# FFN norm with the halves of the channels added on GpSimd, and the constant places of q and k set on GpSimd

## The chip, the cores and the metric

The kernel runs on one core of a Trainium2 chip. All of its arithmetic is fp32. The metric is the device time of one execution in microseconds; the median of several executions is compared. The core's engines are TensorE (PE, with its weight loads as PEld), VectorE (DVE), ScalarE (ACT), GpSimd (POOL) and SyncE (SP), which here only issues DMAs.

## What is computed

The input `x` has 2 sequences of 2048 tokens with 256 channels. It is normalized over the channels, and the result goes through two branches; the output is `x + s * silu(g)`. Cut to what matters:

```python
xn = layernorm(x)
s = global_attention(xn)              # 16 heads of 16, softmax over all 2048 keys, spatial bias
g = silu(ffn_branch(xn))
out = x + s * g

def ffn_branch(x):                    # two layers of:
    x = x + local_attention(shift_token(x)) @ wo      # 8 heads of 64, windows of 128, rotary q and k
    h = shift_token(x)                # second half of the channels comes from the token before
    mu, var = h.mean(-1), h.var(-1)
    h = (h - mu) / sqrt(var + 1e-5) * lg + lb
    a, gate = split(h @ w1 + b1)
    x = x + (a * gelu(gate)) @ w2 + b2
```

The change touches the mean and the variance of `h` in the FFN, and, in the global attention, the places of the q and k tiles that no data fills.

## The kernel before

The program has two stages. `global_attention` comes first; the first product of `ffn_branch` (L736) starts at 1911.0 us.

**Global attention.** The input comes in chunks of 512 tokens, four for each sequence. `xn_pieces` normalizes a chunk (statistics on VectorE, the root on ScalarE for the first sequence, L234) and turns it over on TensorE into `xA[b]`, which holds channels in partitions: `[128, 2, 2049]`, two halves of 128 channels, with a zero column ahead of the tokens. `prep_qk` multiplies by `wk` and `wq`, writes the product to device memory, and `fetch` brings it back so that each head of 16 channels has 32 partitions of its own in `kTs` and `qTs`. Of these 32, 16 hold data. The places between must hold constants: in `kT` a one in place 16 of each 32, against which the maximum is subtracted, and elsewhere zero; in `qT` zero. `set_rest(i)` (L171 to L174) sets a whole pair of tiles before data arrive, by two ScalarE copies of 128x2048, and fills `vs[i]` with ones on GpSimd. The one comes from `ones_col`, a column loaded by a DMA on ScalarE's queue (L154). `set_rest(0)` stands ahead of the first chunk's statistics, `set_rest(1)` after the last chunk's products. Each engine executes its instructions in the order in which the program issues them. ScalarE's queue at the start thus has the DMAs of constants and weights, then `set_rest(0)`, then the first chunk's root. A DMA issue on these queues can wait until an earlier DMA has ended, since they take eight semaphores in turn.

**FFN branch.** The work is cut into 16 slots: two layers, four chunks of 512 tokens, two sequences, in turn. A slot has four tiles of 128 tokens, and one pass of the outer loop (L1050 on) handles one tile. In each pass the pieces go out in an order written by hand:

```python
STEP = "T0 T1 Q S0 S1 V K F G W0 W1 G A0 A1 G".split()
```

Q, K and V are the projections of the current tile. T turns over q and k of the tile before, S scores them, W turns over the weights and A sums with v. G are pieces of the FFN's first matmuls and gates (`f_gate`), of the slot two before. F holds the other pieces of the pass, `xs`: in pass 0 the variance of the slot two before (`f_var`), in pass 1 the projection and residual of the attention of the slot before (`a_out`), in passes 2 and 3 the FFN's output of the slot three before (`f_out`), and in pass 3 the mean of the slot before (`f_mean`). The first nine passes have another order, in which the attention of each tile is finished one pass later. `soon(n, f)` puts a piece off until n further pieces have gone out. It is used where another engine needs time first.

The mean is a matmul with `mean_w`, a 128x128 matrix of 1/256, which gives the sum over partitions on every partition. The two halves of channels are summed in PSUM, two matmuls each for mean (L903) and variance (L917):

```python
for k in range(2):
    nc.tensor.matmul(pm, mean_w, hs[k], start=(k == 0), stop=(k == 1))
```

VectorE then subtracts `pm` from both halves into `hc` (L906), ScalarE squares them into `sq` (L910), and `f_var` sums the squares. The root of the variance (L920), its reciprocal in four pieces (L927) and two scalings per half (L932, L933) follow on ScalarE and VectorE, spread over later pieces.

GpSimd in this stage adds the rotated halves of q and k (L758), takes the power for their norms (L767) and applies it (L768), scales the attention's weights (L840), prepares the rotary tables (L587), and forms the output in layer 2 (L1028, L1029).

Of the kernel before, what the change touches and what calls it, by code (L numbers as in the profile page):

```python
# [11 lines left out]
F32 = mybir.dt.float32  # L12
AF = mybir.ActivationFunctionType
ALU = mybir.AluOpType
AX = mybir.AxisListType
PSUM = bass.MemoryType.PSUM

B, N, D = 2, 2048, 256
P = 128
NT = N // P  # L20
CH = 512
# [5 lines left out]
NG, GH, HD, HP = 4, 4, 16, 32  # L27
NPR, PH = 2, 8
VW = HD + 1
VALL = (PH - 1) * VW + HP  # L30
# [106 lines left out]
def global_attention(tc, t, xA, s_all, s_out, ident, eps_t, x_ch, early):  # L137
# [9 lines left out]
    nc = tc.nc  # L147
    with ExitStack() as ctx:
        cp = ctx.enter_context(tc.tile_pool(name="ga_c", bufs=1))
        p2 = ctx.enter_context(tc.tile_pool(name="ga_2", bufs=2))  # L150
        psr = ctx.enter_context(tc.tile_pool(name="ps_r", bufs=1, space=PSUM))

        ones_col = cp.tile([P, 1], F32, name="ones_col")
        nc.scalar.dma_start(ones_col, t["ones"][:, 2 * P :])  # L154

        w, padded = {}, {}
        for n in ("wk", "wq", "wv"):
# [4 lines left out]
                padded[n, k] = x  # L162
        for n, k in padded:
            nc.gpsimd.tensor_copy(w[n][:, k].rearrange("p (h d) -> p h d", d=HD), padded[n, k][:, :, :HD])

        qTs = [cp.tile([P, N], F32, name=f"qT{i}") for i in range(2)]
        kTs = [cp.tile([P, N], F32, name=f"kT{i}") for i in range(2)]
        vs = [cp.tile([P, NT, VALL], F32, name=f"v{i}") for i in range(2)]
        zero = xA[0][:, 0, 0:1]

        def set_rest(i):  # L171
            nc.scalar.copy(kTs[i], ones_col.to_broadcast([P, N]))
            nc.scalar.copy(qTs[i], zero.to_broadcast([P, N]))
            nc.gpsimd.memset(vs[i], 1.0)  # L174

        dram = ctx.enter_context(tc.tile_pool(name="qk_d", bufs=1, space=bass.MemoryType.DRAM))
        qk_d = {}
# [312 lines left out]
        def both(a, b):  # L490

            n = max(len(a), len(b))
            for i in range(n):
                for x in (a, b):
                    for f in x[i * len(x) // n : (i + 1) * len(x) // n]:
                        f()
# [2 lines left out]
        turns = [firsts[c][0][3:] + firsts[c][1] for c in range(NCH)]  # L499
        preps = [first_preps(c) for c in range(NCH)]  # L500
        maxima = [[(lambda j=j: max_piece(j)) for _ in range(TPC) for j in range(GH)] for _ in range(NCH + 1)]
        set_rest(0)
        both(stat[0], [])
        both(turns[0], stat[1])
        both(preps[0] + turns[1], stat[2])
        both(preps[1] + turns[2], stat[3])
        both(maxima[0], preps[2] + turns[3])
        both(maxima[1], preps[3])
        set_rest(1)
        rest = [lambda: next(sb) for _ in range(4)] + prep[3 * NCH :]  # L510
        both(maxima[2] + maxima[3], rest[:-4])
        both(maxima[4][: LEAD * GH], [lambda: others.pop(0)()] + rest[-4:])
# [141 lines left out]
def ffn_branch(tc, t, xA, s_out, weights, ident, eps_t, mean_w, vecs, b2_row, x_ch, out_ch):  # L654
# [7 lines left out]
    nc = tc.nc  # L662
    with ExitStack() as ctx:
        cp = ctx.enter_context(tc.tile_pool(name="ff_c", bufs=1))
        pool = ctx.enter_context(tc.tile_pool(name="ff", bufs=2))
# [12 lines left out]
        def bank(name, shape=(P, CH)):  # L678
            turn[0] += 1
            return psr.tile(list(shape), F32, tag=f"f{turn[0] % 8}", name=name)  # L680
# [4 lines left out]
        def soon(n, f):  # L685
            later.append([n, f])
# [29 lines left out]
        def release(kind, b):  # L716
            if (kind, b) in held:
                cc, h = held.pop((kind, b))
                at = (cc + 1) * CH
                nc.vector.tensor_copy(xA[b][:, 1, at : at + 1], h)  # L720


        slots = [(l, b, cc) for l in range(DEPTH) for cc in range(NCH) for b in range(B)]
# [171 lines left out]

        fs = {}

        def f_mean(s):
            l, b, cc = slots[s]
            hs = [xA[b][:, k, cc * CH + 1 - k : (cc + 1) * CH + 1 - k] for k in range(2)]  # L900
            pm = bank(f"pm_{s}")
            for k in range(2):
                nc.tensor.matmul(pm, mean_w, hs[k], start=(k == 0), stop=(k == 1))  # L903
            hc = pool.tile([P, 2, CH], F32, tag="hc", name=f"hc_{s}")
            for k in range(2):
                nc.vector.tensor_sub(hc[:, k, :], hs[k], pm)  # L906
            release("f", b)
            sq = pool.tile([P, 2, CH], F32, tag="sq", name=f"sq_{s}", bufs=1)
            fs[s] = {"hc": hc, "sq": sq, "u": []}
            soon(1, lambda: nc.scalar.activation(sq, hc, AF.Square))  # L910

        def f_var(s):
            l, b, cc = slots[s]
            hc, sq = fs[s]["hc"], fs[s]["sq"]
            pw = bank(f"pv_{s}")
            for k in range(2):
                nc.tensor.matmul(pw, mean_w, sq[:, k, :], start=(k == 0), stop=(k == 1))  # L917
            rs = pool.tile([P, CH], F32, tag="rs", name=f"rs_{s}", bufs=1)
            def root():
                nc.scalar.activation(rs, pw, AF.Sqrt, bias=eps_t)  # L920
                for q in range(TPC):
                    soon(2 * q + 1, lambda q=q: invert(q))
                soon(2 * TPC + 2, lambda: scale(0))
                soon(2 * TPC + 3, lambda: scale(1))

            def invert(q):
                nc.vector.reciprocal(rs[:, q * P : (q + 1) * P], rs[:, q * P : (q + 1) * P])  # L927

            def scale(k):
                c0 = 2 * NM + k  # L930
                V = vecs[:, l, :]
                nc.vector.tensor_mul(hc[:, k, :], hc[:, k, :], rs)  # L932
                nc.vector.tensor_scalar(  # L933
                    hc[:, k, :], hc[:, k, :], V[:, c0 : c0 + 1], V[:, c0 + 2 : c0 + 3], ALU.mult, ALU.add
                )
                fs[s]["ready"] = k == 1

            gates.append(root)
# [103 lines left out]
        def out_pieces(s, k):  # L1042
            return [(lambda p=p: f_out(s, k, p)) for p in range(2)]

        def gate_pieces(s):
            return [(lambda m=m, n=n: f_gate(s, m, n)) for m in range(NM) for n in (1, 0)][:-1]
# [3 lines left out]
        for n in range(len(tiles) + 4):  # L1050
            s, i = divmod(n, TPC)
# [5 lines left out]
            def have(x):  # L1057
                return 0 <= x < n_slots


            xs = []
            if s == n_slots:
                if i == 1:
                    xs = [lambda: a_out(s - 1, 0), lambda: a_out(s - 1, 1)] + out_pieces(s - 3, 0)
                    xs += [lambda: f_mean(s - 1)]
                    gq += gate_pieces(s - 2)
                elif i == 2:
                    xs = out_pieces(s - 3, 1) + [lambda: f_var(s - 1)]
                elif i == 3:
                    xs = []  # L1070
                else:
                    xs = [lambda: f_var(s - 2)]
                ng = (5, 2, 5, 5)[i]
            else:
                if i == 0 and have(s - 2):
                    xs = [lambda: f_var(s - 2)]
                if i == 1 and have(s - 1):
                    xs = [(lambda k=k: a_out(s - 1, k)) for k in range(2)]
                if i == 1 and have(s - 2):
                    gq += gate_pieces(s - 2)  # L1080
                if i >= 2 and have(s - 3):
                    xs = out_pieces(s - 3, i - 2)
                if i == 3 and have(s - 1):
                    xs = xs + [lambda: f_mean(s - 1)]
                ng = (5, 2, 3, 2)[i]
# [45 lines left out]
        s = n_slots + 1  # L1131
# [104 lines left out]
```

## Time and profile before

| | |
|---|---|
| median of 3 runs | 3373.33 us (3373.11 to 3376.05) |
| profiled execution | 3379.4 us, span 3377.6 us |
| granted TensorE clock, mean | 0.987 |
| busy PE / PEld | 3298.3 us (98%) / 1630.2 us (48%) |
| busy DVE / ACT / POOL | 2313.2 (68%) / 2093.4 (62%) / 1104.9 us (33%) |
| L903, mean, 128x512 | x64 records |
| L917, variance, 128x512 | x64 records |
| HBM read / written | 36.63 / 16.78 MB |

The profile shows one execution. Its lines name the engine, the line of the kernel, the operation, the tile written and the tiles read, and the shape; "x4" counts instructions. "idle before" tells what released an engine after it had stood idle. The busy time of TensorE is modelled at the end of each matmul, since matmuls overlap, so starts are compared where a length matters. A matmul of fp32 operands in the program appears as two records. Queues that issue DMAs have a q behind the name (ACTq).

### The profile page before, as it was taken

Reading aid. Unit: us, or ns where it says so; the run is one execution under the profiler, and the core shown is the slowest. Engines: PE = TensorE matmul, PEld = TensorE weight load, DVE = VectorE, ACT = ScalarE, POOL = GpSimd, SP = SyncE. Lnnn points to the kernel's source line nnn. Section 1 sums busy time; section 2 is a strip of 40 time slices with the busy share of each in tenths; the row PEclk is TensorE's granted clock in tenths of the full one; section 3 lists DMA queues with packets and bytes.
Section 4 is the critical chain, followed back from the end, with each engine's and each line's share of the span. In section 5 each row is a group of like instructions: output and inputs, shape, how many; then the busy total and the mean of one; then the engine's idle time right before and its main releaser. Section 6 shows DMA issues by size and latency. Waiting matters only on the chain. (4 is left out here: it accounts for less than half of the span.)

```text
span 3377.6 us, 55228 instructions
## 1 busy us (share of the span) xinstructions
PE 3298.3 (98%) x21216; PEld 1630.2 (48%) x21216; DVE 2313.2 (68%) x4978; ACT 2093.4 (62%) x4237; POOL 1104.9 (33%) x951
## 2 busy tenths in 40 slices
PE   6999999999999999999999889999999999999999
PEld 3444444444444444444444355555555555666665
DVE  3798788878777777787786266666666666665642
ACT  3477677667776667767777566555555555555552
POOL 2011111111111111111111365555555555556541
PEclk8899999999999999999999899999999999999999
DMA  2100000000000100000000100000000000000001
GB/s 91 53 1 5 23 1 14 14 13 14 7 18 21 46 14 1 3 12 1 1 1 14 64 9 1 7 1 7 1 1 32 1 19 15 20 20 19 20 20 50
DMA packets 40954, 56.95 MB, mean 17 GB/s; under 512 B 10016, under 2 KB 25460, under 8 KB 40692
## 3 DMA queue, kind: packets, MB, share of 16 engines
q1 hardware_dynamic: 38354, 51.05, 4.7%
q8 instruction: 168, 2.75, 0.3%
q10 hardware_dynamic: 1826, 2.12, 0.2%
q14 instruction: 94, 0.77, 0.1%
q0 software_dynamic: 512, 0.26, 0.0%
HBM read 36.63 MB, written 16.78 MB: 16 GB/s over the span
## 5 line engine op out<-in xcount | busy, mean ns | idle before, releaser
L364 DVE TENSOR_REDUCE mx<-pm 128x1 f32<-128x512 f32 x2048 | 1272.9, 683 | 354.3 <-PE ps L397 308.9
L403 ACT ACTIVATE e<-ps 128x512 f32<-128x512 f32 x2048 | 1069.7, 602 | 259.2 <-PE ps L397 180.2
L361 PE MATMUL pm<-kT,qT 32*128 32x512 f32 x4096 | 1166.3, 626 | 3.6 <-DVE mx L364 3.6
L397 PE MATMUL ps<-qa,kT 32*128 32x512 f32 x4096 | 1110.4, 626 | 14.1 <-ACT e L403 14.0
L427 POOL TENSOR_TENSOR o<-o,part 128x512 f32<-128x512 f32 x224 | 283.8, 1267 | 1450.4 <-ACT part L426 1440.1
L361 PEld LDWEIGHTS pm<-kT,qT 32*128 32x128 f32 x4096 | 487.0, 186 | 374.3 <-DVE mx L364 264.1
L397 PEld LDWEIGHTS ps<-qa,kT 32*128 32x128 f32 x4096 | 442.8, 185 | 212.9 <-ACT e L403 141.5
L416 PE MATMUL po<-e,v 128*32 128x512 f32 x4096 | 497.4, 604 | 1.7 <-DVE mx L364 1.7
L736 PE MATMUL pp<-weights,xA 128*128 128x512 f32 x768 | 361.6, 606 | 0.8 <-DVE s L471 0.8
L758 POOL TENSOR_TENSOR rot<-rot,swp 128x512 f32<-128x512 f32 x128 | 166.8, 1303 | 465.3 <-DVE swp L755 464.7
L954 PE MATMUL pg<-hc,weights 128*128 128x512 f32 x640 | 298.5, 597 | 1.1 <-DVE hc L933 1.1
L416 PEld LDWEIGHTS po<-e,v 128*32 128x32 f32 x4096 | 107.8, 110 | 353.4 <-DVE mx L364 182.3
L426 ACT COPY part<-po 128x512 f32<-128x512 f32 x224 | 131.2, 585 | 224.6 <-PE po L416 223.8
L826 ACT ACTIVATE sm<-sm,wmx 128x256 f32<-128x256 f32 (+1 forms) x512 | 249.6, 489 | 5.5 <-DVE wmx L818 4.5
L767 POOL TENSOR_TENSOR rn<-rn,mhalf 128x8 f32<-128x8 f32 x128 | 210.8, 1647 | 97.5 <-DVE rn L766 92.4
L757 ACT ACTIVATE sqq<-pp 128x512 f32<-128x512 f32 x128 | 76.4, 597 | 262.1 <-DVE swp L755 262.1
L840 POOL TENSOR_TENSOR sm<-sm,wls 128x512 f32<-128x512 f32 (+1 forms) x224 | 222.8, 1026 | 12.1 <-DVE wls L832 12.1
L736 PEld LDWEIGHTS pp<-weights,xA 128*128 128x128 f32 x768 | 136.7, 192 | 130.7 <-issue 122.4
L818 DVE CUSTOM_DVE_ANT_0 sm<-ps,mask 128x256 f32<-128x256 f32 (+1 forms) x512 | 181.3, 410 | 1.1 <-PE ps L805 1.0
L954 PEld LDWEIGHTS pg<-hc,weights 128*128 128x128 f32 x640 | 114.9, 190 | 122.8 <-issue 113.2
L786 DVE COPY xT<-pt 128x512 f32<-128x512 f32 x64 | 43.3, 677 | 155.2 <-PE pt L780 155.1
L805 PEld LDWEIGHTS ps<-xT,xT 64*128 64x128 f32 x1984 | 115.8, 188 | 47.9 <-issue 41.8
(157 smaller groups left out, 3520.1 us busy)
## 6 DMA issues: line engine op xcount, KB each, us to landing
s<-in_x_dram SPq DMA_DIRECT2D x8, 512.0 KB, 5.0
qk_wk<-stage_wk SPq DMA_DIRECT2D x16, 256.0 KB, 2.0
kT<-qk_wk SPq DMA_DIRECT2D x128, 32.0 KB, 1.8
qk_wq<-stage_wq SPq DMA_DIRECT2D x16, 256.0 KB, 2.0
qT<-qk_wq SPq DMA_DIRECT2D x128, 32.0 KB, 1.8
s_out<-s SPq DMA_DIRECT2D x8, 512.0 KB, 2.7
s<-s_out SPq DMA_DIRECT2D x16, 256.0 KB, 3.6
x<-in_x_dram SPq DMA_DIRECT2D x16, 256.0 KB, 3.6
```

Source lines behind the costliest of these rows:

```text
L361: nc.tensor.matmul(ps, qT[rows, q0 : q0 + P], kT[rows, c * CH : (c + 1) * CH], start=True, stop=True)
L364: nc.vector.tensor_reduce(mxs[n][:, i * GH + j, c : c + 1], ps, AX.X, ALU.max)
L397: nc.tensor.matmul(ps, kT[rows, kt * P : (kt + 1) * P], qas[n][rows, :], start=True, stop=True)
L403: nc.scalar.activation(e, ps, AF.Exp)
L416: nc.tensor.matmul(pos[n][j * HP : (j + 1) * HP, :], v[:, kt, (r + j) * VW : (r + j) * VW + HP], es.pop((n, kt, j)), start=(kt % 2 == 0), ...
L427: nc.gpsimd.tensor_add(os[n], os[n], part)
L736: nc.tensor.matmul(ps, xA[b][:, k, at : at + P], W["qkv"][:, k, n * INNER : (n + 1) * INNER], start=(k == 0), stop=(k == 1),)
L767: nc.gpsimd.tensor_tensor(rn, rn, mhalf, ALU.pow)
L818: nc.vector.tensor_tensor_reduce(sm[:, x, lo:], pss[r][:, x, lo:], mask[:, lo:], -1.0, 3e38, ALU.add, ALU.min, mx[:, hb, r, x : x + 1],)
L826: nc.scalar.activation(sm[:, x, lo:], sm[:, x, lo:], AF.Exp, scale=-1.0, bias=mx[:, hb, r, x : x + 1], accum_out=ls[:, hb, r, x : x + 1],)
L840: nc.gpsimd.tensor_mul(sm, sm, ls[:, hb, r, :, None].to_broadcast([P, 2, 2 * P - lo]))
L954: nc.tensor.matmul(ps[:mw], W["1"][:, k, at : at + mw], hc[:, k, :], start=(k == 0), stop=(k == 1))
```

## The change

In the FFN's norm, `f_add` adds the two halves of the channels on GpSimd, into the first half of the tile `hc`, one pass ahead of the mean. The mean is then one matmul with `mean_w`. The subtraction writes `hc` as before. Behind the square, GpSimd adds the two halves of `sq` in place, and the variance is one matmul too. In the last passes of the program, `f_add` stands between the attention's residual and the output pieces of the same pass.

At the beginning, `ones_col` is no longer loaded: VectorE sums the columns 16, 48, 80 and 112 of the identity. `qTs[0]` is set by a GpSimd memset, `kTs[0]` by a GpSimd copy of `ones_col`, both ahead of the copies of the weights; `vs[0]` is filled after them. The second pair and `vs[1]` are set on GpSimd too. A first small square root on ScalarE (`root_table`) stands ahead of the DMAs of the weights. In the order of the changed program the second pair follows GpSimd's 16 DMA issues of `wp`. The packed last tile of the FFN (`f_last`) is in both versions.

```diff
         ones_col = cp.tile([P, 1], F32, name="ones_col")
-        nc.scalar.dma_start(ones_col, t["ones"][:, 2 * P :])
+        nc.vector.tensor_reduce(ones_col, ident[:, HD::HP], AX.X, ALU.add)
+        root_table = cp.tile([P, 1], F32, name="root_table")
+        nc.scalar.activation(root_table, eps_t, AF.Sqrt)
+
+        qTs = [cp.tile([P, N], F32, name=f"qT{i}") for i in range(2)]
+        kTs = [cp.tile([P, N], F32, name=f"kT{i}") for i in range(2)]
+        vs = [cp.tile([P, NT, VALL], F32, name=f"v{i}") for i in range(2)]
+        nc.gpsimd.memset(qTs[0], 0.0)
+        nc.gpsimd.tensor_copy(kTs[0], ones_col.to_broadcast([P, N]))
...
         for n, k in padded:
             nc.gpsimd.tensor_copy(w[n][:, k].rearrange("p (h d) -> p h d", d=HD), padded[n, k][:, :, :HD])
-
-        qTs = [cp.tile([P, N], F32, name=f"qT{i}") for i in range(2)]
-        kTs = [cp.tile([P, N], F32, name=f"kT{i}") for i in range(2)]
-        vs = [cp.tile([P, NT, VALL], F32, name=f"v{i}") for i in range(2)]
-        zero = xA[0][:, 0, 0:1]
-
-        def set_rest(i):
-            nc.scalar.copy(kTs[i], ones_col.to_broadcast([P, N]))
-            nc.scalar.copy(qTs[i], zero.to_broadcast([P, N]))
-            nc.gpsimd.memset(vs[i], 1.0)
+        nc.gpsimd.memset(vs[0], 1.0)
+
+        def set_rest():
+            nc.gpsimd.tensor_copy(kTs[1], ones_col.to_broadcast([P, N]))
+            nc.gpsimd.memset(qTs[1], 0.0)
+            nc.gpsimd.memset(vs[1], 1.0)
...
-        set_rest(0)
         both(stat[0], [])
...
-        set_rest(1)
+        set_rest()
...
+        def halves(s):
+            l, b, cc = slots[s]
+            return [xA[b][:, k, cc * CH + 1 - k : (cc + 1) * CH + 1 - k] for k in range(2)]
+
+        def f_add(s):
+            hs = halves(s)
+            hc = pool.tile([P, 2, CH], F32, tag="hc", name=f"hc_{s}")
+            nc.gpsimd.tensor_add(hc[:, 0, :], hs[0], hs[1])
+            fs[s] = {"hc": hc}
+
         def f_mean(s):
             l, b, cc = slots[s]
-            hs = [xA[b][:, k, cc * CH + 1 - k : (cc + 1) * CH + 1 - k] for k in range(2)]
+            hs = halves(s)
             pm = bank(f"pm_{s}")
-            for k in range(2):
-                nc.tensor.matmul(pm, mean_w, hs[k], start=(k == 0), stop=(k == 1))
-            hc = pool.tile([P, 2, CH], F32, tag="hc", name=f"hc_{s}")
+            nc.tensor.matmul(pm, mean_w, fs[s]["hc"][:, 0, :], start=True, stop=True)
+            hc = fs[s]["hc"]
             for k in range(2):
                 nc.vector.tensor_sub(hc[:, k, :], hs[k], pm)
...
             soon(1, lambda: nc.scalar.activation(sq, hc, AF.Square))
+            soon(2, lambda: nc.gpsimd.tensor_add(sq[:, 0, :], sq[:, 0, :], sq[:, 1, :]))
...
-            for k in range(2):
-                nc.tensor.matmul(pw, mean_w, sq[:, k, :], start=(k == 0), stop=(k == 1))
+            nc.tensor.matmul(pw, mean_w, sq[:, 0, :], start=True, stop=True)
...
-                    xs += [lambda: f_mean(s - 1)]
+                    xs = xs[:2] + [lambda: f_add(s - 1)] + xs[2:] + [lambda: f_mean(s - 1)]
...
+                if i == 2 and have(s - 1):
+                    xs = [lambda: f_add(s - 1)] + xs
                 if i == 3 and have(s - 1):
                     xs = xs + [lambda: f_mean(s - 1)]
```

## The prediction

> **What bounds the kernel now.** I read the page first for the engine shares and the 40 slices, then the busy time by stretches, then the waits of TensorE in the FFN stage, and last the order of time at the three places that the diff touches: the first 20 us, the statistics steps of one slot, and GpSimd around them.
>
> Busy time by stretches (us, then for PE, PEld, DVE, ACT, POOL the busy us and instruction count, then granted clock, DMA share, GB/s):
>
> ```profile
> 0.00:20.00 20.00, 0.75 (x2) 0.36 (x2) 3.81 (x16) 8.01 (x8) 8.27 (x31) 1.00 0.68 214
> ...
> 2400.00:2700.00 300.00, 300.00 (x1608) 167.31 (x1607) 183.83 (x499) 165.32 (x379) 164.63 (x141) 1.00 0.03 10
> ```
>
> In the FFN stage TensorE is busy in all of the 300 us, at full clock, while VectorE, ScalarE and GpSimd work 55 to 61% of the time; from 2700 to 3000 us it reads alike. A busy PE can hide waits, so I ask for them (us in all, times, longest), from 1950 to 3338 us:
>
> ```profile
> PE pt L780 <- POOL rot L768: 5.8, 4, 2.1
> PE px L889 <- ACT oT L882: 4.6, 2, 3.9
> PE pw L853 <- POOL sm L840: 2.0, 7, 0.3
> PE pg L954 <- DVE hc L933: 1.1, 1, 1.1
> ```
>
> With two entries of 0.2 us that is 13.9 us in 1388 us. What stands in TensorE's queue there is the time: taking a matmul out of it takes out its length, and another engine's extra work is free as long as it does not make one of these rows grow. Now the statistics steps of a slot and their length on TensorE (start us, us):
>
> ```profile
> 2534.05 5.51 PE L995 MATMUL py<-u,w 128*128 128x512 f32 x12
> 2539.49 1.98 PE L903 MATMUL pm<-xA,mean_w 128*128 128x512 f32 x4
> 2541.31 1.88 PE L954 MATMUL pg<-hc,weights 128*128 128x512 f32 x4
> ...
> 2556.75 1.88 PE L917 MATMUL pv<-sq,mean_w 128*128 128x512 f32 x4
> 2558.46 3.60 PE L954 MATMUL pg<-hc,weights 128*128 128x512 f32 x8
> ```
>
> Durations overlap, so the start-to-start time is what a matmul costs: pv's four records take 2558.46 - 2556.75 = 1.71 us, 0.43 each. A 128x512 fp32 matmul of the program is two records (768 records at L736 for 384 matmuls), 0.86 us.
>
> The start is another matter: there TensorE waits for ScalarE, which issues DMAs until 11.5 us and then works through four items before the first square root:
>
> ```profile
> 11.51 1.28 ACT L172 ACT_TABLE_LOAD   x1 [11.51 <-DMA wq<-in_wq_dram]
> 12.80 1.90 ACT L172 COPY kT<-ones_col 128x2048 f32<-128x2048 f32 x1
> 14.60 1.89 ACT L173 COPY qT<-xA 128x2048 f32<-128x2048 f32 x1
> 16.51 1.28 ACT L234 ACT_TABLE_LOAD   x1
> 17.81 0.30 ACT L234 ACTIVATE rs<-mv,eps_t 128x4 f32<-128x4 f32 x1
> ```
>
> VectorE's reciprocal at 18.14 comes after 10.94 us of idle time for that root, and TensorE's first instruction comes at 19.22.
>
> **The change, part by part.**
>
> *Matmuls taken out.* Each of 16 slots loses one of two matmuls in the mean (L903) and one of two in the variance (L917): 32 matmuls, 64 records, at 0.43: 64 x 0.43 = 27.5 us. The group table divides busy time instead: 29.1 us / 60 records = 0.485, or 31 us for 64; 0.43 excludes overlap, so I take it and keep 31 as the upper end.
>
> *GpSimd adds.* Each slot gains two 128x512 fp32 adds. The nearest row is the same operation on the same shape, L758 `rot<-rot,swp`: 1.27 to 1.30 us. So 32 x 1.3 = 42 us more for an engine that works 165 us of 300. In the order of the changed program the first add (`hc`) comes one pass after the attention residual and one pass ahead of the mean's matmul; in place it lies between K's `rot` add and K's `rn`. The slot of 2600 us:
>
> ```profile
> 2601.97 1.26 POOL L758 TENSOR_TENSOR rot<-rot,swp 128x512 f32<-128x512 f32 x1
> 2603.34 1.65 POOL L767 TENSOR_TENSOR rn<-rn,mhalf 128x8 f32<-128x8 f32 x1
> 2605.06 1.04 POOL L768 TENSOR_TENSOR rot<-rot,rn 128x512 f32<-128x512 f32 x1
> ```
>
> Its operand is long ready (the residual ended by 2584), so it waits for nothing. Queued behind it are `rn` and `rot`, which would end at 2607.4 in place of 2606.1; who waits is the transpose `pt`, at 2611.54. Cover: 4 us. Cost nothing; if that cover were gone, 1.3 us in each of 16 slots, 21 us. The second add (`sq`) waits for ScalarE's Square. At 2542.83 + 1.07 the square is done, GpSimd has a table product until 2545.6, so the add ends by 2546.9; behind it the next `rot` add starts at 2552.83, and the variance's matmul at 2556.75. Cover: 6 and 10 us. In layer 2 the output's two products stand ahead of it (3074.43 to 3077.06), so it ends near 3078.3; the matmul is at 3089.37. At the very end (mean at 3294.71, square done at 3301.3) the add ends at 3302.6, the matmul starts at 3306.72 and will start about 1 us earlier: 3 us of cover.
>
> *Where the cover fails.* Slot 0 runs while the other order of pieces holds (until about 2040 us). There Square ends at 2031.87, but the next `rot` add began at 2031.39: with the new add between, the `rot` behind it starts near 2033.2, 1.8 us late, and the transpose at 2043.42 had 3.1 us after `rot` ended at 2040.3. TensorE would come 1.7 us earlier; and `pw` at 2040.67 already stretches to 2.91 us on ScalarE's normalization. I give slot 0 back: 1 us. FFN: 27.5 - 1 = 26.5 us.
>
> *The port.* VectorE's product with two operands in SBUF, `rn<-ss,tiny` (128x8):
>
> ```profile
> 2532.06 0.17 DVE L766 TENSOR_TENSOR rn<-ss,tiny 128x8 f32<-128x8 f32 x1
> ...
> 2539.04 1.27 DVE L766 TENSOR_TENSOR rn<-ss,tiny 128x8 f32<-128x8 f32 x1
> ```
>
> The long one coincides with GpSimd's `rot` add of 2539.03 for its whole length. The Trainium skill says why (SBUF — State Buffer, Who interferes with whom): a VectorE instruction with two SBUF inputs and a GpSimd instruction that reads SBUF block each other, the loser for the winner's whole instruction. That speaks against this change: 32 more GpSimd reads of 1.27 us each can hold VectorE up, to 40.6 us by the rule. By the trace VectorE pays this in every pass already, and TensorE waited for it 1.3 us in all (the row of `hc` above and one of the small entries); at 2603 the next thing TensorE needs of VectorE is the copy of `pw` (2604.90, after 0.98 us of idle; it feeds `po` at 2607.82), so 1.27 us of blocking leaves it 0.3 us late with over 1 us to spare. By the rule alone charged to the end, the FFN stage would be 26.5 - 40.6 = 14 us longer; by the trace nothing. I take nothing.
>
> *The start.* Gone from ScalarE: the DMA of `ones_col` (0.52 us), both copies, the first table load; the root's table load moves ahead of the weight DMAs, with one small root: 1.28 + 0.30. What remains between the last DMA issue and the root is nothing, so 17.81 - 11.51 = 6.3 us are freed, if issuing ends when it did. It ends with `bpr`, which waits for a finished DMA: before for the first of `wq`, after (one DMA fewer in the rotation) for the second of `wk`, which GpSimd took up at 10.48. The weights are issued 1.58 - 0.52 = 1.06 us later. So the root comes between 10.9 and 12.9 us, gain 4.9 to 6.9; I take 5.8. On GpSimd the memset of `qT` (row: 2.13 us for 2416 elements, so 1.8) and the copy of `kT` come ahead of the weight copies; `kT` waits for `ones_col`, reduced on VectorE after the first chunk's statistics, at 7.2. The copy of 2048 is not in the trace: between a memset (1.8) and four 512-element two-operand products (5.1); by the row of the same operation, 0.40 us for 256, 3.2. So the `wk` copies end at 11.3 to 13.1; the first product that needs them stands at 21.92, near 16 after. Cover: 3 us or more. `v`'s memset moves ahead of `wp`'s 8 us of DMA issues, and is done near 18, against 26.9 before; its reader, ScalarE's copy at 29.80, moves to 24. The second `kT`, `qT` (84.17 to 87.87 on ScalarE) follow those issues, done near 34 us, and are first written at about 130. ScalarE's freed 3.8 us at 84 hold up only the bias pieces, for which VectorE idled 0.31 us: 0.3.
>
> Sum: 26.5 + 5.8 + 0.3 = 32.6 us. The profiled execution took 3379.4 (span 3377.6), so 3346.8 by its own time; the median before is 3373.33, 6.1 below it, so 3340.7, said as 3341.
>
> **The rivals.**
>
> *The start's gain does not carry on (0.17).* DMAs are the limit there (68% share), and the weights come later; or the half-speed matmuls of that stage (`pp_wk`, weight loads 0.85 us apart from 22.9 to 25.5, 0.43 after) fall otherwise. Against: after the root all is a chain of ScalarE, TensorE and fetches with no fixed time in it. Then 26.8 is left: 3346.5.
>
> *Half of the FFN gain is given back (0.12).* GpSimd's adds make `pt` and `pw` late (rows L780, L853 above grow). At half, 13 us: 3354.
>
> *Slower: blocking reaches TensorE (0.05).* Mechanism: each GpSimd add takes the port just ahead of VectorE's `rn` or `hc` instruction, VectorE's copies of `pw` and `pt` come late, and TensorE stands. Price: all 32 x 1.27 = 40.6 us, against 27.5 + 6.1 saved: 7 us slower, 3380. It decides only if over 33.6 of the 40.6 us reach TensorE, over 1 us per add. Against: VectorE idles 4.44 us ahead of one transposed copy (2549.61).
>
> *More (0.06).* 31 us of matmuls and 6.9 at the start: 3373.3 - 37.9 = 3335.
>
> That the change does not do what it says is excluded by its order of instructions: each `pm` and `pv` group has one matmul instead of two, and nothing else on TensorE differs.
>
> **The numbers.** My case has 0.60, with a range of its own from 3336 to 3346. A difference under 0.2% (6.7 us) can hardly be told here. Faster by more: all but the slower rival and a thin edge, 0.92; within: 0.03; slower: 0.05. The range from 3332 to 3351 takes in the first rival and the larger gain, and leaves out the half gain and the slower case.
>
> **What would show it.** Right: L903 and L917 at x32 records each; the waits of TensorE in the FFN stage within 5 us of 13.9; the root near 12 us and TensorE's first instruction near 13.5; new GpSimd rows `hc<-xA` and `sq<-sq`, x16, 1.3 us. Wrong: a row of TensorE waiting on `hc` or `sq` from GpSimd, or `pt <- POOL rot` well over 6 us; VectorE's `hc` scaling or `rn` rows longer with TensorE idle behind them; or a first transpose still after 17 us.

## The result, and the profile after

The changed kernel took 3338.97 us (median of 4 runs, 3338.0 to 3347.47), the kernel before on the same chip 3374.53; the ratio is 0.99, 95% interval 0.9883 to 0.9917. The forecast was 3341, in a range from 3332 to 3351. The profiled execution took 3338.83 us, span 3337.0, so it is 40.6 us below the profiled one of before. By the medians the gain is 35.6 us, near the forecast's 32.6, but its parts are not, and one of them was not in the forecast at all. The medians here and below leave out two executions, of 3746.63 us (`before_shift`) and 11060.77 us (the kernel before, in the same session).

First the busy time by stretches of the changed kernel (us, then busy us and count of PE, PEld, DVE, ACT, POOL, then granted clock, DMA share, GB/s):

```profile
0.00:20.00 20.00, 5.47 (x13) 2.83 (x14) 6.23 (x27) 5.23 (x10) 11.33 (x29) 1.00 0.71 211
2400.00:2700.00 300.00, 300.00 (x1634) 167.93 (x1633) 187.36 (x509) 168.88 (x386) 176.75 (x152) 1.00 0.03 10
```

TensorE is still busy in all of the 300 us; GpSimd has gone from 165 to 177. The new and the halved instructions, from the views by tile (ns min/median/max, first and last start):

```profile
L916 PE MATMUL pm<-hc,mean_w x32: 592/592/697, 2007.8 to 3256.2; 128*128 128x512 f32 x32
L924 POOL TENSOR_TENSOR sq<-sq x16: 1262/1270/1279, 2014.3 to 3261.6; 128x512 f32<-128x512 f32 x16
```

The mean has x32 records instead of x64, and an addition takes 1.27 us, as the row of `rot` said. One steady slot in order of time (start us, us):

```profile
2515.17 1.12 PE L916 MATMUL pm<-hc,mean_w 128*128 128x512 f32 x2
2516.13 1.88 PE L967 MATMUL pg<-hc,weights 128*128 128x512 f32 x4
...
2531.57 1.02 PE L930 MATMUL pv<-sq,mean_w 128*128 128x512 f32 x2
2532.43 3.60 PE L967 MATMUL pg<-hc,weights 128*128 128x512 f32 x8
```

The variance now holds TensorE for 2532.43 - 2531.57 = 0.86 us; before it was 1.71. The waits of TensorE from 1950 to 3338 us (us in all, times, longest):

```profile
PE px L893 <- ACT oT L886: 4.6, 2, 3.9
PE pw L857 <- POOL sm L844: 2.9, 9, 0.3
PE pt L784 <- POOL rot L772: 2.9, 2, 2.1
PE pw L857 <- ACT sm L841: 2.0, 1, 2.0
```

With two of 0.2 us that is 12.8 us, against 13.9 before. Here `pw` are the attention's weights as TensorE turns them over, and `sm` the same weights as ScalarE or GpSimd normalizes them; `rot` are q or k after the rotation, `rn` their norms, `pt` are q or k as TensorE turns them over, `po` the sums with v, `px` their projection. No row waits on `hc` or `sq` from GpSimd. But the row of ScalarE's `sm` is new, and it is one wait of 2.0 us. Last, the start on ScalarE:

```profile
12.19 0.34 ACTq L189 DMA_DIRECT2D bet<-in_ln_beta_dram  x1
12.56 0.44 ACTq L191 DMA_DIRECT2D bpr<-in_b_proj_dram  x1
13.06 0.30 ACT L239 ACTIVATE rs<-mv,eps_t 128x4 f32<-128x4 f32 x1 [9.78 <-DMA wq<-in_wq_dram]
```

The root comes as soon as the DMA issues end, but they end at 13.0 us. Split at instructions that both kernels have, the 40.6 us are:

| stretch | before | after | gain | forecast |
|---|---|---|---|---|
| start to first root | 17.8 | 13.1 | 4.7 | 5.8 |
| root to first score (`ps`) | 116.4 | 110.5 | 5.9 | 0.3 |
| first score to first `po` | 17.8 | 17.7 | 0.1 | 0 |
| first `po` to last `po` | 1748.6 | 1743.1 | 5.5 | 0 |
| last `po` to first FFN product | 10.4 | 9.7 | 0.7 | 0 |
| FFN, to the end | 1466.6 | 1442.9 | 23.7 | 26.5 |

So the FFN gave 3 us less than thought, the root 1 us less, and the attention from the root to the last `po`, in which the change was to move nothing beyond the bias pieces, gave 11.5.

### The profile page after: what moved, and what is told of

The parts are those of the page before. It is cut to its first block, busy times and chain, and to the rows that moved or that the text cites. A ratio compares the mean times of both kernels' runs of the same rounds, so it can differ in the third digit from the quotient of the medians.

```text
span 3337.0 us, 55149 instructions
## 1 busy us (share of the span) xinstructions
PE 3261.9 (98%) x21152; PEld 1614.2 (48%) x21152; DVE 2312.9 (69%) x4979; ACT 2085.5 (62%) x4233; POOL 1152.7 (35%) x987
## 5 line engine op out<-in xcount | busy, mean ns | idle before, releaser
L967 PEld LDWEIGHTS pg<-hc,weights 128*128 128x128 f32 x640 | 115.0, 190 | 121.3 <-issue 116.0
```

What stands on the lines that cost most here:

```text
L967: nc.tensor.matmul(ps[:mw], W["1"][:, k, at : at + mw], hc[:, k, :], start=(k == 0), stop=(k == 1))
```

## The experiments

Medians, each with the kernel before on the same chip; the last four columns are from the profile:

| kernel | us | before | ratio (95%) | root | root to score | `po` first to last | FFN |
|---|---|---|---|---|---|---|---|
| start_only | 3368.19 | 3376.23 | 0.9972 [0.9965, 0.9979] | 13.4 | 114.1 | 1744.7 | 1467.2 |
| ffn_only | 3353.14 | 3376.23 | 0.9934 [0.9922, 0.9947] | 18.0 | 116.3 | 1746.9 | 1441.6 |
| after_again | 3344.6 | 3376.23 | 0.9905 [0.9892, 0.9919] | 13.8 | 116.0 | 1741.5 | 1442.9 |
| s0_var2 | 3345.59 | 3376.23 | 0.9909 [0.9896, 0.9923] | 13.3 | 114.5 | 1744.7 | 1443.1 |
| double_adds | 3345.46 | 3377.64 | 0.9898 [0.9881, 0.9914] | 13.6 | 114.7 | 1744.7 | 1442.6 |
| early_root | 3338.77 | 3377.64 | 0.9886 [0.9871, 0.99] | 7.4 | 117.2 | 1742.5 | 1441.5 |
| start_delay | 3346.08, one run | 3377.64 | | 15.7 | 116.1 | 1742.5 | 1441.4 |
| before_again | 3377.15, one run | 3377.64 | | 17.5 | 114.6 | 1748.3 | 1466.7 |
| before_shift | 3373.27 | 3375.65 | 0.9991 [0.9982, 1.0001] | 17.8 | 116.3 | 1744.9 | 1466.8 |
| ones_dma | 3344.09 | 3375.65 | 0.9912 [0.9897, 0.9926] | 12.7 | 110.9 | 1745.3 | 1443.2 |
| fills_act | 3350.59 | 3375.65 | 0.9925 [0.9908, 0.9942] | 17.4 | 114.5 | 1742.0 | 1443.0 |

### The two parts alone, and the whole again

`start_only` is the changed kernel with the FFN's code of before; `ffn_only` has the beginning of before and the changed FFN; `after_again` is the changed kernel once more.

> Only the beginning of the change (constants on GpSimd, root table early); the FFN is as before. Theory A (the beginning is worth its chain of waits and, on top, TensorE's half-speed matmuls that fall away as its work closes up): 10 to 11 us faster than before, ratio 0.997, root near 13 us, first attention score (L397 before) near 123.6 instead of 134.2. Theory B (the prediction's: only the chain, 6.1 us): score near 128, ratio 0.998.

> Only the FFN part of the change. Theory A (slot 0 loses 4 us to a stall and a fallen clock, the other 15 slots gain all of 1.72 us): 23.7 us faster than before, ratio 0.993; the stretch from the first FFN product to the end is 23 to 24 us shorter. Theory B (slot 0 gives back only its own 1 us, the shortfall is spread over all slots): the stretch is 26.5 us shorter, or the shortfall is not at one place.

> The changed kernel once more, on the same chip as the others. If the 5.5 us by which the steady global attention (first weighted sum to last) was shorter in its profile is only the spread between executions, a second profile has that stretch anywhere between 1743 and 1749 us. If the change itself shortened it, it is again 1743.

The parts gained 8.0 and 23.1 us by their medians, together 31.1; the whole gained 31.6 in the same session. They add up, so neither part lives off the other. In `start_only` the first score came at 127.5 us, so the beginning was worth its chain of waits alone (theory B). In `ffn_only` neither theory held: the FFN was 25.0 us shorter, and slots 1 and 14 lost as well as slot 0, as shown below.

The repeat also showed where the first profile is better. From 60 to 120 us the first profile of the changed kernel, and then the repeat:

```profile
60.00:120.00 60.00, 57.14 (x222) 24.53 (x222) 38.83 (x66) 11.57 (x22) 0.00 (x0) 0.94 0.14 49
```

```profile
60.00:120.00 60.00, 57.14 (x205) 24.70 (x205) 35.66 (x60) 10.97 (x21) 0.00 (x0) 0.83 0.13 45
```

Same program, same busy share, but a granted clock of 0.94 against 0.83, and 222 matmuls against 205. One product shows the size, first as it stands in the repeat, then in the first profile:

```profile
65.41 3.78 PE L298 MATMUL pp_wk<-xA,wk 128*128 128x512 f32 x4
```

```profile
62.09 1.99 PE L298 MATMUL pp_wk<-xA,wk 128*128 128x512 f32 x4
```

It takes twice as long where the clock is half. The whole times fall into two groups: `start_only` has 7 of 21 runs from 3361.8 to 3364.0 and 14 from 3367.2 to 3371.0; the changed kernel, with its repeat, has four from 3337.7 to 3339.1 and four from 3344.2 to 3347.5. The mean granted clock of each run parts them in the same way, 0.990 in the quick ones and 0.987 or 0.988 in the others. That the clock is lost between 60 and 120 us is seen in the profiled runs alone. The Trainium skill (TensorE: Matmul & The Clock Gate, Part 1) says that the monitor behind the clock looks through a window that runs free of the program, so one kernel can show different slow counts from run to run; that fits, though no run here shows the window. Of the 5.9 us from root to first score, then, most is how that execution fell: in the other eight profiles with the new start the stretch takes 110.9 to 117.2 us, in the four with the old start 114.6 to 116.4.

### Do the additions cost anything?

`double_adds` issues each of the two new GpSimd additions twice, the second one of the squares into the half that nothing reads any more:

```diff
             nc.gpsimd.tensor_add(hc[:, 0, :], hs[0], hs[1])
+            nc.gpsimd.tensor_add(hc[:, 0, :], hs[0], hs[1])
...
             soon(2, lambda: nc.gpsimd.tensor_add(sq[:, 0, :], sq[:, 0, :], sq[:, 1, :]))
+            soon(2, lambda: nc.gpsimd.tensor_add(sq[:, 1, :], sq[:, 0, :], sq[:, 1, :]))
```

> The change, with both GpSimd adds of each slot done twice (the second square add writes the half of the tile that nothing reads): 32 more adds, 41 us of GpSimd time. Theory A (the adds are covered by GpSimd's idle time and by the distance to their readers): slots 2 to 15 take the same 1.72 us less than before, the stretch from the first FFN product to the end grows by 0 to 3 us, at slots 0 and 1 only. Theory B (the adds reach TensorE through the blocking of VectorE, and the cover is thin): each slot is longer by up to 1.3 us, 10 to 40 us in all.

GpSimd in a steady slot of it:

```profile
2499.93 1.27 POOL L909 TENSOR_TENSOR hc<-xA 128x512 f32<-128x512 f32 x1
2501.27 1.28 POOL L910 TENSOR_TENSOR hc<-xA 128x512 f32<-128x512 f32 x1
...
2525.88 1.28 POOL L925 TENSOR_TENSOR sq<-sq 128x512 f32<-128x512 f32 x1 [0.30 <-ACT sq L924]
2527.23 1.27 POOL L926 TENSOR_TENSOR sq<-sq 128x512 f32<-128x512 f32 x1
```

32 more additions are 41 us of GpSimd work, and the FFN takes 1442.6 us against 1442.9. From one mean to the next every slot but slot 0 takes what it took in `after_again`, within 0.05 us (86.62 in most); slot 0 takes 70.4 against 70.8. So outside slot 0 the cover is real, and there is as much again of it.

### Where the 3 us of the FFN went

From one mean to the next, most slots gained 1.71 to 1.73 us, two matmuls at 0.86. Three did not. I took slot 0 first, since the new wait is there, and left its variance at two matmuls, without the addition of squares:

```diff
-            soon(2, lambda: nc.gpsimd.tensor_add(sq[:, 0, :], sq[:, 0, :], sq[:, 1, :]))
+            if s:
+                soon(2, lambda: nc.gpsimd.tensor_add(sq[:, 0, :], sq[:, 0, :], sq[:, 1, :]))
...
-            nc.tensor.matmul(pw, mean_w, sq[:, 0, :], start=True, stop=True)
+            for k in range(1 if s else 2):
+                nc.tensor.matmul(pw, mean_w, sq[:, k, :], start=(k == 0), stop=(k == 1 or s > 0))
```

> The change, but in slot 0 alone the variance stays two matmuls and GpSimd adds no squares. Theory A (the add of the squares in slot 0, between the queue's rot additions, holds VectorE and ScalarE up until TensorE stands and its clock falls): TensorE's wait for ScalarE's normalized weights near 2022 us goes from 1.96 to under 1 us, the granted clock there stays 1.00, and the time falls by 3.2 us (4.1 lost, less the 0.86 of the matmul put back) against the change: 3335.7. Theory B (the stall there has another cause, the matmul's missing 0.86 us alone): 0.9 us slower than the change or the same.

The whole time did not fall by 3.2 us: 3345.59 against 3344.6, but runs in two groups 7 us apart cannot show so little. In its profile TensorE's wait for ScalarE's `sm` is gone and the clock stays at 1.00, as theory A had it. Slot 0 took 71.0 us, against 72.4 in the first profile of the changed kernel but 70.8 in the repeat, which has the addition too. What differs between those two is a race on VectorE. First the first profile, VectorE and then GpSimd:

```profile
2015.57 1.29 DVE L770 TENSOR_TENSOR rn<-ss,tiny 128x8 f32<-128x8 f32 x1
```

```profile
2014.34 1.27 POOL L924 TENSOR_TENSOR sq<-sq 128x512 f32<-128x512 f32 x1 [2.78 <-ACT sq L923]
2015.57 1.27 POOL L762 TENSOR_TENSOR rot<-rot,swp 128x512 f32<-128x512 f32 x1
```

and then the repeat, in the same order:

```profile
2022.51 0.17 DVE L770 TENSOR_TENSOR rn<-ss,tiny 128x8 f32<-128x8 f32 x1
```

```profile
2021.29 1.28 POOL L924 TENSOR_TENSOR sq<-sq 128x512 f32<-128x512 f32 x1 [2.80 <-ACT sq L923]
2022.53 1.30 POOL L762 TENSOR_TENSOR rot<-rot,swp 128x512 f32<-128x512 f32 x1
```

Where VectorE wins, its product takes 0.17 us. Where it loses it takes 1.29, all of GpSimd's instruction. The maxima on VectorE, then ScalarE's normalization, come 1.1 us late, and TensorE stands before `pw`; the first profile, then the repeat:

```profile
2023.87 3.51 PE L857 MATMUL pw<-ident,sm 128*128 128x128 f32 x16 [1.96 <-ACT sm L841]
```

```profile
2029.48 3.23 PE L857 MATMUL pw<-ident,sm 128*128 128x128 f32 x16 [0.63 <-ACT sm L841]
```

Behind the longer wait the granted clock falls, in all three profiles that have it; the first one:

```profile
2025.00:2030.00 5.00, 5.00 (x21) 3.64 (x21) 1.53 (x3) 4.97 (x11) 0.00 (x0) 0.66 0.00 0
```

In the other ten, with a wait of 0.6 us or none, the clock there is 1.00. The race exists since the change, because the new addition pushes `rot` to the very moment of `rn`: without it (`s0_var2`) `rot` starts 2.5 us ahead of `rn`, with two additions (`double_adds`) 1.4 us behind, and `rn` takes 0.17 us in both. In the profiles it was lost in the changed kernel, `ones_dma` and `fills_act` (slot 0: 72.4 to 72.5 us) and won in `after_again`, `early_root` and `start_delay` (70.8) and in `ffn_only` (71.1): 1.6 us, wait and clock together. In all seven the two starts lie within 0.02 us of each other, and their recorded order does not tell who wins: `rot` is recorded 0.006 us ahead in the changed kernel, but behind by 0.006 and 0.009 in `ones_dma` and `fills_act`, which lost too, and within 0.001 in three that won. And in slot 0 a variance matmul is worth little even with the race won, for TensorE waits for ScalarE there.

Slot 1 gained 0.85 of 1.72, slot 14 0.86. There TensorE, 0.86 us earlier, meets the pace of GpSimd's weight products (`sm`), one in 1.00 us; this is read from the trace, and no run tests it. Slot 1 in `after_again`:

```profile
2088.09 1.16 PE L857 MATMUL pw<-ident,sm 128*128 128x128 f32 x8
2089.59 0.66 PE L857 MATMUL pw<-ident,sm 128*128 128x128 f32 x4 [0.34 <-POOL sm L844]
2090.59 0.66 PE L857 MATMUL pw<-ident,sm 128*128 128x128 f32 x4 [0.34 <-POOL sm L844]
```

Before, the same place had one such wait, of 0.17 us. In slot 14 `pw` and what follows it stretch from 2.77 us (3271.93 to 3274.70) to 3.49. For slot 0 like must be compared with like: it takes 71.35 us in the two profiles of before, but 71.0 in `start_only` and `before_shift`, which have one small VectorE instruction more at their start. With the race won the FFN's change shortens it by 0.2 us (`before` to `ffn_only`, and `start_only` to `after_again`), with it lost it lengthens it by 1.4. So what is given back of 1.72 us a slot is 1.5 or 3.1 us in slot 0, 0.87 in slot 1 and 0.86 in slot 14: 3.2 to 4.8 us, not 1.

The stretch ahead of the first mean, from which no matmul was taken, differs between profiles too, from 113.7 to 115.2 us. `start_only` and `after_again` have it alike, and there the FFN gains 24.2 us; `before` and `ffn_only` give the same 24.2 without that stretch. The 23.7 of the first profile is a lost race and a quick stretch ahead of it.

### The start

`early_root` takes the first root off the weights: `wv` is loaded on SyncE's queue, and `gam`, `bet` and `bpr` behind the input there. `start_delay` puts three ScalarE copies of 128x512 ahead of the first root.

```diff
-                nc.scalar.dma_start(x, t[n][:, k].rearrange("p (h d) -> p h d", d=HP))
+                (nc.sync if n == "wv" else nc.scalar).dma_start(x, t[n][:, k].rearrange("p (h d) -> p h d", d=HP))
...
+        for v, n in ((gam, "ln_gamma"), (bet, "ln_beta"), (bpr, "b_proj")):
+            nc.sync.dma_start(v, t[n][None, :].to_broadcast([P, D]))
```

```diff
...
+        for _ in range(3):
+            nc.scalar.copy(delay, eps_t.to_broadcast([P, CH]))
         both(stat[0], [])
```

> The change, with the DMAs of wv, gamma, beta and the projection's bias issued on SyncE's queue instead of ScalarE's. Theory A (after the change the root waits for nothing but the queue's last DMA issues, which wait for the weights to land): the root comes when VectorE's statistics are done, near 7.5 us instead of 13.1 to 13.8; TensorE's first transpose near 9 us; its first product then waits for wk near 12.5 us instead of starting at 17.2: 4 us gained there, if wq and wv land in time. Theory B (the transfers bound the start, 3.5 MB at the rate they have): the products move by under 1 us.

> The change, with three ScalarE copies of 128x512 (about 1.5 us, to a tile that nothing reads) put back ahead of the first root. Theory A (from root to first attention score the time hangs on where TensorE's half-speed stretches fall, 110.5 to 116.4 us in the profiles so far): root 1.5 us later, and the first score anywhere from 125 to 132 us. Theory B (a fixed chain, 110.5 us): the first score 1.5 us after 123.6 to 129.8, and root to score within 0.5 us of the change's own.

> The kernel before once more. If the half-speed stretches of the start fall by chance from execution to execution, root to first score (116.4 us in the first profile and 116.3 in the run with the old start) can be shorter here, down to 110; if they belong to the old order of work, it is 116 again. The steady attention stretch is expected between 1741 and 1749 us.

In `early_root` the root comes at 7.40, 5.7 us earlier, and the first score only at 124.6. In the four profiles with the changed start and a clock of 0.83 to 0.85 from 60 to 120 us it comes at 127.5 to 129.8, in the two with 0.94 (the changed kernel's first and `ones_dma`) at 123.6. The first product shows what stops it:

```profile
11.02 1.89 POOL L163 COPY kT<-ones_col 128x2048 f32<-128x2048 f32 x1 [6.65 <-DVE ones_col L155]
12.86 0.74 POOL L173 COPY wk<-wk 128x256 f32<-128x256 f32 x2
13.31 3.78 PE L295 MATMUL pp_wk<-xA,wk 128*128 128x512 f32 x4 [1.72 <-POOL wk L173]
```

TensorE waits for `wk`, behind the copy of `kT` on GpSimd, which waits for `ones_col`; VectorE makes that at 10.81 us now, among the second chunk's statistics, instead of 7.11. The cover for GpSimd's work at the start is used up. All four runs lie between 3338.58 and 3338.86. Against 3344.6 of the changed kernel's repeat that is better by 6 us, against its first median no difference; the intervals of the two ratios overlap (0.9871 to 0.99, and 0.9892 to 0.9919 for the repeat), so it is not shown to be quicker. It is the steadiest of the versions, in four runs. `start_delay` moved the root by 2 us, and its one run, 3346.08, lies among the changed kernel's slower four, so it cannot tell its two theories apart. `before_again` repeats the kernel before: 114.6 us from root to score, 1.8 less than the first profile of the same kernel, and 1748.3 from first to last `po`, against 1748.6.

`fills_act` gives ScalarE its copies back, for both pairs, and keeps the rest of the new start:

```diff
-        nc.gpsimd.memset(qTs[0], 0.0)
-        nc.gpsimd.tensor_copy(kTs[0], ones_col.to_broadcast([P, N]))
...
+        def set_rest(i):
+            nc.scalar.copy(kTs[i], ones_col.to_broadcast([P, N]))
+            nc.scalar.copy(qTs[i], zero.to_broadcast([P, N]))
+            nc.gpsimd.memset(vs[i], 1.0)
...
```

> The changed kernel with the constant places of q and k set by ScalarE copies as before, and vs filled on GpSimd behind the weights as before; root_table, the sum for ones_col and the FFN are the changed kernel's. It splits what the beginning is worth. Theory: the two copies stand ahead of the root again, 3.79 us, so the root comes near 16.9 (13.1 in the changed kernel, 17.8 before); the other 1 us of the root's gain is the table load and the small DMA. If GpSimd's fills cost anything where they now stand, the stretch from root to first score is shorter here than in the changed kernel; as nothing there waits for them, it should be 114 to 117 us, as in the other runs. Rival: the ScalarE copies are covered, since the root waits for the input's statistics anyway, and the root stays near 13.5. In the end 3348 by the theory in the usual runs, 3344 by the rival.

```profile
13.32 0.44 ACTq L189 DMA_DIRECT2D bpr<-in_b_proj_dram  x1
13.81 1.90 ACT L175 COPY kT<-ones_col 128x2048 f32<-128x2048 f32 x1 [10.53 <-DMA wv<-in_wv_dram]
15.61 1.89 ACT L176 COPY qT<-xA 128x2048 f32<-128x2048 f32 x1
17.41 0.29 ACT L237 ACTIVATE rs<-mv,eps_t 128x4 f32<-128x4 f32 x1
```

The root is back at 17.4; in the two profiles of before it is 17.8 and 17.5. So the copies are nearly all of what the root gained, and moving the table load (1.28 us twice before, once ahead of the weights now) gained 0.1 to 0.4: issuing ends at 13.8 instead of 11.5.

### The attention's 4 us

The part between first and last `po` has no changed instruction, yet it is shorter in every profile with the new start than in those of before. A unit of this attention is 512 queries of four heads, and there are 32. From the maximum of one unit to that of the next, two intervals part the kernels: the third, 53.7 us in `before`, `before_again` and `ffn_only` but 52.5 in the seven profiles with the new start taken up to then, and the fifth, 59.8 but 56.9. The others agree within 0.3 us, except for falls of the granted clock of 0.4 to 6.0 us, which come between the ninth unit and the end of the last, at other units from profile to profile, in kernels of both kinds. In the first pair these are 4.8 us in the changed kernel and 6.0 in the one before. So of the 5.5 us between first and last `po`, 4.1 are the two intervals and 1.3 are where the falls came.

The third, on VectorE, GpSimd and in TensorE's waits from 225 to 300 us, in the kernel before:

```profile
231.96 0.47 DVE L281 SCALAR_TENSOR_TENSOR s<-s,mvs,gam 128x256 f32<-128x256 f32 x1
232.89 1.44 DVE L282 SCALAR_TENSOR_TENSOR s<-s,rss,bet 128x256 f32<-128x256 f32 x1 [0.46 <-DVE s L281]
```

```profile
232.78 1.27 POOL L427 TENSOR_TENSOR o<-o,part 128x512 f32<-128x512 f32 x1 [1.20 <-ACT part L426]
```

```profile
PE pn L374 <- DVE mx L364: 1.1, 1, 1.1
```

The same race again. VectorE pauses 0.46 us, for which the profile names only its own last product; GpSimd's addition gets in first; VectorE's product takes 1.44 us for 0.48; the maxima behind it are late, and TensorE waits 1.1 us. In the changed kernel it runs through:

```profile
221.28 0.47 DVE L286 SCALAR_TENSOR_TENSOR s<-s,mvs,gam 128x256 f32<-128x256 f32 x1
221.86 0.48 DVE L287 SCALAR_TENSOR_TENSOR s<-s,rss,bet 128x256 f32<-128x256 f32 x1
```

```profile
222.11 1.36 POOL L432 TENSOR_TENSOR o<-o,part 128x512 f32<-128x512 f32 x1 [1.19 <-ACT part L431]
```

Nothing in the change is near. What it does to VectorE's program in this stage is to put one instruction more at its start, the sum for `ones_col`. Two kernels part that from the rest: `before_shift` adds such an instruction to the kernel before, into a tile that nobody reads, and `ones_dma` takes it out of the changed kernel.

```diff
         nc.scalar.dma_start(ones_col, t["ones"][:, 2 * P :])
+        spare = cp.tile([P, 1], F32, name="spare")
+        nc.vector.tensor_reduce(spare, ident[:, HD::HP], AX.X, ALU.add)
```

```diff
-        nc.vector.tensor_reduce(ones_col, ident[:, HD::HP], AX.X, ALU.add)
+        nc.scalar.dma_start(ones_col, t["ones"][:, 2 * P :])
```

> The kernel before with one small VectorE instruction more at its start: the sum of four columns of the identity that the changed kernel has, into a tile nobody reads. Nothing else differs. In three kernels with the old start, VectorE pauses 0.46 us ahead of one normalization product (s<-s,rss,bet, near 232 us), then loses 0.96 us to a GpSimd addition (1.44 us instead of 0.48), TensorE waits 1.1 us, and the third attention unit takes 53.7 us instead of 52.5. The fifth takes 59.8 instead of 56.9, with the granted clock down to 0.81 and 0.51. In seven kernels with the new start neither is there. Theory A, it hangs on where an instruction stands in VectorE's program: the product takes 0.48 us here, the third unit 52.5, and if the clock's fall follows from that pause, the fifth 56.9; the time is 1 to 4 us below the kernel before. Rival B, it hangs on when the stage starts or on GpSimd's and ScalarE's work at the beginning: 1.44, 53.7 and 59.8 as before, same time. The measurement of the whole time is hardly fine enough, so the unit intervals decide.

> The changed kernel with ones_col loaded by a DMA on ScalarE's queue, as before, instead of summed on VectorE. VectorE's program in the attention stage is then that of the kernel before; all the rest is the changed kernel's. Theory A (place in VectorE's program): the product s<-s,rss,bet takes 1.44 us and the third unit 53.7, perhaps the fifth 59.8; the time is 1 to 4 us above the changed kernel's. Rival B (time of the start, or the constants set on GpSimd): 0.48, 52.5 and 56.9 as in the changed kernel. The DMA issue adds about 0.5 us on ScalarE ahead of the root, which should come near 13.6.

VectorE in `before_shift`, then in `ones_dma`:

```profile
232.49 0.49 DVE L284 SCALAR_TENSOR_TENSOR s<-s,rss,bet 128x256 f32<-128x256 f32 x1
```

```profile
222.23 1.44 DVE L287 SCALAR_TENSOR_TENSOR s<-s,rss,bet 128x256 f32<-128x256 f32 x1 [0.46 <-DVE s L286]
```

The pause follows the instruction, not the start: the third interval is 52.5 in `before_shift` and 53.7 in `ones_dma`. In all four profiles with the pause a packet of queue q14, of the kind "instruction", starts 1.1 us after the pause began; in the nine without it the nearest one starts over 9 us earlier. So the pause goes with a shift in the fetch of instructions. But the packet starts when the pause is over, so VectorE did not wait for this packet; the mechanism is not shown.

The fifth interval is a fall of the clock. The kernel before at 360 to 368 us:

```profile
360.00:362.00 2.00, 1.80 (x7) 1.35 (x11) 2.00 (x5) 1.23 (x3) 0.00 (x0) 0.78 0.09 23
362.00:364.00 2.00, 2.00 (x9) 0.33 (x1) 1.81 (x5) 1.57 (x3) 0.00 (x0) 0.50 0.59 132
364.00:366.00 2.00, 2.00 (x13) 0.59 (x16) 1.97 (x6) 0.60 (x1) 0.00 (x0) 0.50 1.08 377
```

It is there in the three profiles with the old start and the old VectorE program, and in none of the ten others. `ones_dma` has the pause without the fall, and `before_shift` the old start without it, so neither alone brings it about. Nor do the waits ahead of it: TensorE waits 0.87 us for ScalarE 5 us before the fall and 0.41 us at it, and all thirteen profiles have these two waits at the same place in the unit. What does stays open.

## Why the prediction was right or wrong

**FFN matmuls, 64 records at 0.43: right.** 12 slots gained 1.71 to 1.73 us each. The alternative of 31 us, by divided busy time, would be 1.94 a slot and is refuted.

**"GpSimd adds: cost nothing": right outside slot 0.** No wait on `hc` or `sq`, and twice the additions cost nothing either.

**"I give slot 0 back: 1 us": the step that failed most.** It should have read 3.2 to 4.8. In slot 0 I had seen the order of the queues and missed that the shift brings GpSimd's `rot` onto VectorE's `rn`. Slots 1 and 14 I passed over because `pw <- POOL sm` was a small row, 2.0 us in seven waits. But a small wait is the sign that TensorE runs level with GpSimd: take TensorE work out ahead of it and the wait grows. The row is 2.9 us after; the two slots lost 1.7.

**"The port: I take nothing": right for the sum, incomplete as an argument.** In the steady slots it cost nothing; the rule that the loser waits for the winner's instruction held for VectorE where the two met (1.29 us for 0.17 in slot 0); GpSimd as the loser lost less (1.36 us for 1.27 in the attention, beside a VectorE product with 0.23 us to go). But I asked only about new blocking. The old program was paying 1.2 us for one such meeting in the attention, and the change removed it by chance.

**The start, 5.8 for the root: 4.7 in this profile, 4.0 in the repeat.** The 3.79 us of the copies came nearly whole. Of the 2.5 us for table load and small DMA about 1 came here and 0.1 to 0.4 in `fills_act`, because the queue's issues, which are what the root then waits for, ended at 13.0, past the upper end of my 10.9 to 12.9. My reason for a later end, "the weights are issued 1.06 us later", was not what happened. First the kernel before, then the changed one:

```profile
2.33 1.18 ACTq L161 DMA_DIRECT2D wk<-in_wk_dram  x2
```

```profile
1.78 1.28 ACT L157 ACT_TABLE_LOAD   x1 [1.78 <-issue]
1.85 1.40 ACTq L170 DMA_DIRECT2D wk<-in_wk_dram  x2
```

`wk` was issued 0.5 us earlier, while the table loaded, and still landed later: GpSimd made its last copy at 11.8 instead of 10.5. What I had left out is SyncE's queue. Its waits up to 14 us in the kernel before have this row:

```profile
SPq L226 <- DMA ones_col<-in_ones_dram: 4.5, 1, 4.5
```

The last load of the input stood in turn behind the DMA of `ones_col` and waited for it. With that DMA gone the input's loads were issued by 4.6 us instead of 9.4. All nine profiles with the new start have the third load of the input at 1.8 us and the first half of `wk` landed at 10.6 to 11.3; all four with the old start have 4.2 to 4.4 and 9.3 to 9.7. So the input probably took the weights' place; no run tests that alone. `gam`, `bet` and `bpr` then wait for these DMAs to end. "After the root all is a chain with no fixed time in it" is not true either: with the root at 7.4 TensorE met `wk`.

**The copy of `kT` on GpSimd, 3.2 us by the nearest row of the same operation:** 1.89, at the lower bound of what I gave.

**What the sum left out:** 4.1 us in the attention (1.2 by the race, 2.9 by the clock), and a clock that moves the whole by 7 us from run to run. In the repeat the whole gained 31.6 us, near 32.6, because the 4.1 fill the place of what the FFN (2.3) and the root (1.8) gave less. That is luck. That the median came within 2 us of the forecast is owed in part to three quick runs of four, and that is luck too.

## What to carry to other kernels

When work is taken from the bounding engine, look for places where it already waits a little for another one, however small the row: there the gain ends. When work is moved to GpSimd, check what VectorE instruction with two SBUF operands stands at the moment to which the queue behind it moves; where the two start within 0.02 us of each other, either may win, and 1.1 us hang on it. When a DMA is taken out, look which issues waited in turn behind it: they now come earlier and compete with the rest. And before a gain or a loss of a few microseconds is put down to an edit, run a kernel with one harmless instruction more: here that was worth 4 us of the profile, more than the difference between some of the parts; the whole times could not show it.

## What was not expected

One small instruction at the start of VectorE's program, 0.14 us long, removes a wait over 200 us later and, with the old start, a fall of the clock 130 us after that. The whole times do not show it (3373.27 against 3375.65, interval of the ratio 0.9982 to 1.0001); only the intervals between units do. TensorE's clock fell to half (0.50) at 362 us with no wait longer than 0.9 us in the 30 us ahead of it, so it does not need a long stall, and with the same waits it did not fall there in ten other profiles.
